# Attention: the products with the greatest score, of four heads in one pass of a step's first set

## The chip, the cores and the metric

The kernel runs on one core of one Trainium2 chip. Its time is device time in microseconds (us), from the start to the end of one execution. The engines of the core work side by side, each through its own list of instructions in order: PE (TensorE, matrix products; its weight loads are shown apart as PEld), DVE (VectorE), ACT (ScalarE), POOL (GpSimd), and SP, which issues most of the DMAs. Matrix products end in PSUM, which has eight banks here of 512 float32 columns by 128 partitions.

## The reference

A small hybrid model, all in float32, for 4 batches of 1024 positions of width 256:

```
x = x + attention(layernorm(x))
x = x + cell(layernorm(x))        # gated recurrence, 64 steps
x = x + deltanet(layernorm(x))
x = x + cell(layernorm(x))

# attention: 16 heads, causal
q_lat = einsum('bqhd,hdl->bhql', q, k_eff)
attn  = softmax(where(causal, einsum('bhql,bkl->bhqk', q_lat, c_kv) / sqrt(hs), -inf))
y     = einsum('bhqk,bkl->bhql', attn, c_kv), then v_eff by heads
```

Only the attention is touched by the change.

## The kernel before, in words

The attention (`attention`, L39 on) fills about the first half of the time, from 19.7 us, when the first scores are multiplied, to about 673 us. What follows it (`feed_and_delta`) is the cell and the deltanet.

The 16 heads of 4 batches are cut into 16 **units** of four heads each (`units`, L66). Each head has 16 numbers to a position; a unit lays its four heads on four row groups of 32 partitions (`rows`, L352). The softmax needs each row's greatest score before the exponentials are taken, so each unit is gone through twice: as `first`, where the scores lie with the queries on the partitions and DVE takes the greatest of each row; and, one unit later, as `second`, where the scores are made again with the keys on the partitions, with the greatest score subtracted by a further product, and ACT takes the exponential out of PSUM into the tile `p`. The loop at L515 runs over i from -1 to 15: unit i+1 is `first` while unit i is `second`. For i from 0 to 14 both are there.

Each round has twelve **steps** (`STEPS`, L52). A step is one block of 128 keys for the one unit, and one block of 128 queries for the other, times n columns: n is 512, 384, 256, 128, then 512 five times, then 384, 256, 128 for the steps 0 to 11. Steps 0 to 3 and 8 to 11 lie on the diagonal. There a product of `identb` and `mb` adds the causal mask for the second unit (L382), and a masked reduction serves the first unit (L407); in steps 4 to 7 the reduction is the plain one at L413.

`quad` (L355) makes a step in two **sets** of four score tiles, one bank each, two of the second unit and two of the first. In this text F0 to F3 are the second unit's tiles of heads 0 to 3 (in the code `False`; "one" is false), whose reader is the exponential on ACT (L403), and T0 to T3 are the first unit's (`True`), whose reader is a reduction on DVE (L407 or L413).

- The first set holds F2, T0, F3, T1; the second F0, T2, F1, T3.
- A set has three **passes** (L384). In the first, each tile gets the product with the high part of the keys (`kh`), in the second that with the low part (`kl`). The four products of a pass lie on four different row groups. In the third pass only the two F tiles get a product, that of `minus` and `gr`, which subtracts the greatest score; in its trace row the products of the second unit are L397 and those of the first unit L388, for all passes.
- Behind the passes stand the four readers (L401 to L415).

Between the two sets of step s stand the products of the exponentials of step s-2 with the values (`values`, L439, matrix products at L447; eight instructions, which use all 128 rows). Behind the second set stand the **woven pieces** (`places`, L525): small parts of other work for PE, each with a tile from the same pool of banks. `greatest` (L423, its product at L427) stands behind steps 0 and 5, `weighed` (L455, four transposes at L461) behind steps 2 and 6. In nine of the rounds pieces of the next batch stand behind steps 1 and 3 to 9: layernorm and `turn` (L232), `latent` (L246), `feature` (L267), `vals` (L256); in some later rounds a few of the next layer's (L232, L343).

All these tiles come from one pool of seven banks (`pss`, L63); the eighth bank holds the values' sum (`pys`). A tile takes a bank that has come free, and the first product into it waits until the reader of the tile that had it is through. The order of the instructions on each engine is the order in which the code stands (`tc.manual_schedule`, L479).

Of the kernel before, what the change touches and what calls it, by code (L numbers as in the profile page):

```python
# [10 lines left out]
F32 = mybir.dt.float32  # L11
BF16 = mybir.dt.bfloat16
F32R = mybir.dt.float32r
AF = mybir.ActivationFunctionType
ALU = mybir.AluOpType
AX = mybir.AxisListType
PSUM = bass.MemoryType.PSUM

P = 128
# [19 lines left out]
def attention(k, w, x):  # L39
# [6 lines left out]
    nc, tc = k.nc, k.tc  # L46
    NT = T // P
    NG = NH // 4
    NU = B * NG
    ROW = HS  # L50

    STEPS = [  # L52
        (3, 0, 512, 0, 0), (2, 0, 384, 0, 1), (1, 0, 256, 0, 2), (0, 0, 128, 0, 3),
        (4, 0, 512, 1, 0), (5, 0, 512, 1, 1), (6, 0, 512, 1, 2), (7, 0, 512, 1, 3),
        (7, 512, 512, 1, 4), (6, 512, 384, 1, 5), (5, 512, 256, 1, 6), (4, 512, 128, 1, 7),
    ]
    with ExitStack() as es:
        wp = es.enter_context(tc.tile_pool(name="a_w", bufs=1))
        big = es.enter_context(tc.tile_pool(name="a_big", bufs=1))
# [2 lines left out]
        pys = es.enter_context(tc.tile_pool(name="a_psy", bufs=1, space=PSUM))  # L62
        pss = es.enter_context(tc.tile_pool(name="a_pss", bufs=7, space=PSUM))  # L63
# [6 lines left out]
        def load(b):  # L70
# [21 lines left out]
        mask = wp.tile([P, 512], F32, name="mask")  # L92
        nc.gpsimd.memset(mask, 0.0)
        nc.gpsimd.affine_select(
            out=mask[:, 384:], in_=mask[:, 384:], compare_op=ALU.is_ge, fill=NEG, base=0,
# [36 lines left out]
        VS = HS + 1  # L132
# [219 lines left out]
        def rows(j):  # L352
            return ds(32 * j, 32)

        def quad(i, s):  # L355


            first = units[i + 1] if i + 1 < NU else None
            second = units[i] if i >= 0 else None
            qt, c0, n, half, kt = STEPS[s]  # L360
            if second is not None:
                p = sm.tile([P, 4, 512], F32, tag="p", name="p", bufs=3)
                second.p[s] = p
                q0 = 512 - n
            if first is not None and s == 0:
                first.m = sm.tile([P, 2, 4, 4], F32, tag="m", name="m")
                first.m0 = sm.tile([P, 4, 4], F32, tag="m0", name="m0")
            kinds = []
            if first is None or second is None:
                kinds.append([(first is not None, j) for j in range(4)])  # L370
            else:
                kinds += [[(False, 2), (True, 0), (False, 3), (True, 1)]]
                kinds += [[(False, 0), (True, 2), (False, 1), (True, 3)]]

            def make(kind):
                tiles = []
                diag = kt >= 4 * half
                for one, j in kind:
                    ps = pss.tile([P, 512], F32, tag="s", name="ps_s1" if one else "ps_s2")
                    tiles.append(ps)  # L380
                    if diag and not one:
                        nc.tensor.matmul(ps[:, 0:P], identb, mb, start=True, stop=True)  # L382
                keys, at = ds(kt * P, P), ds(half * 512 + 512 - n, n)
                for turn_ in range(3):  # L384
                    for (one, j), ps in zip(kind, tiles):
                        r = rows(j)
                        if one and turn_ < 2:
                            nc.tensor.matmul(  # L388
                                ps[:, :n], first.q[r, ds(qt * P, P)], (first.kh, first.kl)[turn_][r, ds(c0, n)],
                                start=turn_ == 0, stop=turn_ == 1,  # L390
                            )
                        elif not one:
                            if turn_ < 2:
                                a, m = (second.kh, second.kl)[turn_][r, keys], second.q[r, at]
                            else:
                                a, m = minus[r, :], second.gr[r, at]
                            nc.tensor.matmul(  # L397
                                ps[:, :n], a, m, start=turn_ == 0 and not diag, stop=turn_ == 2,
                                skip_group_check=diag,
                            )  # L400
                for (one, j), ps in zip(kind, tiles):  # L401
                    if not one:
                        nc.scalar.activation(p[:, j, q0:], ps[:, :n], AF.Exp)  # L403
                        continue
                    if c0 + n == (qt + 1) * P:
                        junk = sm.tile([P, 512], BF16, tag="junk", name="junk")
                        nc.vector.tensor_tensor_reduce(  # L407
                            out=junk[:, :n], in0=ps[:, :n], in1=mask[:, 512 - n :], scale=1.0,
                            scalar=-3e38 if qt < 4 else first.m0[:, j, qt - 4 : qt - 3],
                            op0=ALU.add, op1=ALU.max, accum_out=first.m[:, qt // 4, j, qt % 4 : qt % 4 + 1],  # L410
                        )
                    else:
                        nc.vector.tensor_reduce(  # L413
                            first.m0[:, j, qt - 4 : qt - 3], ps[:, :n], AX.X, ALU.max
                        )  # L415

            make(kinds[0])
            yield
            for kind in kinds[1:]:
                make(kind)  # L420
            yield

        def greatest(i, half):  # L423
# [14 lines left out]

        def values(i, s):  # L439
            u = units[i]  # L440
            _, _, n, half, kt = STEPS[s]
            q0 = 512 - n
            last = kt == 4 * half + 3
            if kt == 0:
                u.y = pys.tile([P, 512], F32, tag="y", name="ps_y")
            for j in range(4):
                nc.tensor.matmul(  # L447
                    u.y[ds(32 * j, 32), q0:], vb[u.b % 2][:, kt, ds((4 * u.g + j) * VS, 32)], u.p[s][:, j, q0:],
                    start=kt == 0, stop=last,
                )  # L450
            if last:
                u.ys = sm.tile([P, 512], F32, tag="ys", name="ys")
                nc.scalar.copy(u.ys, u.y)  # L453
# [24 lines left out]
        LAG = 2  # L478
        with tc.manual_schedule():  # L479
# [35 lines left out]
            for i in range(-1, NU):  # L515

                if i >= 0 and i % NG == 0 and i // NG + 1 < B:
                    rest += of_batch(i // NG + 1)
                if i > NG and i % NG == 1:

                    late += normed(i // NG - 1, True)
                if i == NG + 1:
                    late.append(k.scale_ffn)
                    late += [lambda g=g: first_cells(g) for g in "fic"]
                places = [[] for _ in range(12)]  # L525
                if i < 0:
                    places[0] += rest[:2]
                    places[1] += rest[2:4]
                    for a, f in enumerate(rest[4:]):
                        places[3 + a * 9 // len(rest[4:])].append(f)  # L530
                    rest = []
                else:
                    for work, left in ((rest, NG - 1 - i % NG), (late, NG - i % NG)):
                        share = -(-len(work) // left) if left > 0 else len(work)
                        for a, f in enumerate(work[:share]):
                            places[LONG[a * len(LONG) // share]].append(f)
                        del work[:share]
                if i + 1 < NU:
                    places[5].append(lambda i=i: greatest(i + 1, 0))
                if 0 <= i < NU - 2:  # L540

                    for j in range(4):
                        places[2 + j].append(lambda i=i, j=j: heads(i + 2, j))
                if i >= 0:
                    units[i].p = {}
                    places[0].insert(0, lambda i=i: greatest(i, 1))
                    places[6].insert(0, lambda i=i: weighed(i, 0))
                if i >= 1:
                    places[2].insert(0, lambda i=i: weighed(i - 1, 1))
                for s in range(12):  # L550
                    run = quad(i, s)
                    next(run)
                    at = i * 12 + s - LAG
                    if at >= 0:
                        values(*divmod(at, 12))
                    next(run)
                    for f in places[s]:
                        f()
                if i == 1:
                    k.load_ffn()  # L560
                if i == NG + 2:
                    load(B - 1)
            for at in range(NU * 12 - LAG, NU * 12):
                values(*divmod(at, 12))
            weighed(NU - 1, 1)


# [1034 lines left out]
```

## Time and profile before

| | |
|---|---|
| median of 3 runs | 1350.02 us (1347.22 to 1359.29) |
| the profiled execution | 1350.2 us |
| its span, first to last instruction | 1348.4 us |
| TensorE clock granted in it | 0.985 of full speed on average, 1.00 from 110 to 600 us |
| busy in the span: PE, DVE, ACT, POOL | 1276.7, 851.0, 708.4, 422.3 us |
| busy between 300 and 400 us, in the attention: PE, DVE, ACT, POOL | 98.91, 75.66, 63.57, 20.94 us |
| DMA, share of 16 engines between 300 and 400 us | 0.31 |

Busy PE is not PE at its peak: products on different row groups run side by side, and the time of one, with its way through the array, counts as busy. So in the attention a PE that is 99% busy still contains waits, and they show as idle time ahead of its weight loads. The profile's page gives the busy times, forty slices of the span, the chain of work that ended last and the groups of instructions by line; the timeline gives the start of each instruction.

### The profile page before, as it was taken

To read this page: it belongs to the slowest core of one execution; us is meant where nothing else is said; L and a number is where in the kernel's file an instruction comes from. 1 tells how busy PE (TensorE), PEld (TensorE's weight loads), DVE (VectorE), ACT (ScalarE), POOL (GpSimd) and SP (SyncE) were. 2 spreads that over 40 slices of the span, in tenths; PEclk is the share of its full clock that TensorE was granted. 3 is DMA by queue.
4 is the path that set the end of the run, shared out by engine and by line. 5 is a ranking of instruction groups with operands and counts; after the bars stand their busy time and mean duration, and the time that the engine had idled before them with its cause. 6 is when DMAs were issued, how large, how long until landed. Compare 5 with 4: busy or idle time off the path is not lost. (4 is left out here: it accounts for less than half of the span.)

```text
span 1348.4 us, 36845 instructions
## 1 busy us (share of the span) xinstructions
PE 1276.7 (95%) x14596; PEld 773.9 (57%) x14596; DVE 851.0 (63%) x2440; ACT 708.4 (53%) x1754; POOL 422.3 (31%) x681
## 2 busy tenths in 40 slices
PE   7899999999999999999899989989888999999997
PEld 3444454444554444444444766756555677777886
DVE  6776778777787777788122345467978867434333
ACT  3266666566666666666732366445565543334332
POOL 1040002323032020022000136445888844535220
PEclk9799999999999999999999999989999999999999
DMA  3723712334221233220030123313555432333210
GB/s 111 187 50 81 198 50 61 60 88 144 66 54 50 97 92 66 66 50 4 25 97 6 47 63 90 102 40 110 139 145 137 132 99 71 106 90 100 63 63 32
DMA packets 118652, 112.25 MB, mean 83 GB/s; under 512 B 46672, under 2 KB 103504, under 8 KB 118480
## 3 DMA queue, kind: packets, MB, share of 16 engines
q1 hardware_dynamic: 95200, 100.39, 27.7%
q10 hardware_dynamic: 23280, 9.51, 2.7%
q8 instruction: 115, 1.88, 0.6%
q14 instruction: 57, 0.47, 0.1%
HBM read 65.22 MB, written 44.63 MB: 81 GB/s over the span
## 5 line engine op out<-in xcount | busy, mean ns | idle before, releaser
L403 ACT ACTIVATE p<-ps_s 128x512 f32<-128x512 f32 (+3 forms) x768 | 334.4, 491 | 209.6 <-PE ps_s L397 208.3
L388 PE MATMUL ps_s<-kh,q 32*128 32x512 f32 (+3 forms) x768 | 220.9, 438 | 10.0 <-DMA q<-qall 4.7
L413 DVE TENSOR_REDUCE m<-ps_s 128x1 f32<-128x512 f32 x256 | 163.8, 682 | 26.3 <-PE ps_s L388 26.1
L397 PE MATMUL ps_s<-q,kh 32*128 32x512 f32 (+3 forms) x768 | 176.9, 438 | 0.0
L388 PE MATMUL ps_s<-kl,q 32*128 32x512 f32 (+3 forms) x768 | 169.7, 358 | 0.0
L447 PE MATMUL ps_y<-p,vb 128*32 128x512 f32 (+3 forms) x1536 | 164.1, 500 | 1.4 <-ACT ys L453 1.4
L407 DVE CUSTOM_DVE_ANT_0 junk<-ps_s,mask,m 128x512 bf16<-128x512 f32 (+3 forms) x256 | 129.2, 547 | 48.7 <-PE ps_s L388 36.4
L407 DVE CUSTOM_DVE_ANT_0 junk<-ps_s,mask 128x512 bf16<-128x512 f32 (+3 forms) x256 | 114.6, 486 | 45.4 <-PE ps_s L388 39.1
L397 PE MATMUL ps_s<-q,kl 32*128 32x512 f32 (+3 forms) x768 | 143.0, 370 | 0.0
L397 PE MATMUL ps_s<-gr,minus 32*128 32x512 f32 (+3 forms) x768 | 132.2, 343 | 0.0
L388 PEld LDWEIGHTS ps_s<-kh,q 32*128 32x128 f32 x768 | 100.1, 182 | 43.3 <-DVE m L413 14.3
L397 PEld LDWEIGHTS ps_s<-q,kh 32*128 32x128 f32 x768 | 76.9, 182 | 83.0 <-ACT p L403 20.7
L471 POOL TENSOR_TENSOR xa<-xa,yt 128x256 f32<-128x256 f32 x32 | 23.4, 732 | 277.9 <-DVE yt L467 266.4
L382 PEld LDWEIGHTS <-identb 128*128 128x128 bf16 x512 | 34.6, 98 | 104.0 <-issue 98.7
L388 PEld LDWEIGHTS ps_s<-kl,q 32*128 32x128 f32 x768 | 87.9, 185 | 0.0
L194 POOL TENSOR_SCALAR rs<-mv 128x2 f32<-128x2 f32 x24 | 5.5, 228 | 256.6 <-DVE mv L193 256.6
L1079 DVE SCALAR_TENSOR_TENSOR gate<-gate 128x256 f32<-128x256 f32 (+1 forms) x56 | 29.3, 523 | 77.1 <-ACT gate L1058 77.1
L397 PEld LDWEIGHTS ps_s<-gr,minus 32*128 32x128 f32 x768 | 73.4, 185 | 3.2
L382 PE MATMUL ps_s<-mb,identb 128*128 128x128 bf16 x512 | 72.1, 224 | 0.8 <-ACT vb L257 0.3
L397 PEld LDWEIGHTS ps_s<-q,kl 32*128 32x128 f32 x768 | 71.5, 184 | 0.0
L1039 PE MATMUL ps_gate<-xnT,ffn_wi 128*128 128x256 f32 (+1 forms) x224 | 67.1, 423 | 3.5 <-DVE hh L1152 3.3
L1039 PE MATMUL ps_gate<-xnT,ffn_wf 128*128 128x256 f32 (+1 forms) x224 | 66.9, 422 | 1.3 <-DVE yt L467 1.0
(228 smaller groups left out, 2607.1 us busy)
## 6 DMA issues: line engine op xcount, KB each, us to landing
x<-x SPq DMA_DIRECT2D x30, 512.0 KB
kh<-kall SPq DMA_DIRECT2D x120, 64.0 KB
kl<-kall SPq DMA_DIRECT2D x120, 64.0 KB
q<-qall SPq DMA_DIRECT2D x120, 64.0 KB
kall<-hl SPq DMA_DIRECT2D x14, 512.0 KB
qall<-hl SPq DMA_DIRECT2D x12, 512.0 KB
kept<-gs ACTq DMA_DIRECT2D x32, 192.0 KB
gl<-kept SPq DMA_DIRECT2D x32, 192.0 KB
```

Source lines behind the costliest of these rows:

```text
L194: nc.gpsimd.tensor_scalar(rs, mv[:, :, 1], EPS, None, ALU.add)
L382: nc.tensor.matmul(ps[:, 0:P], identb, mb, start=True, stop=True)
L388: nc.tensor.matmul(ps[:, :n], first.q[r, ds(qt * P, P)], (first.kh, first.kl)[turn_][r, ds(c0, n)], start=turn_ == 0, stop=turn_ == 1,)
L397: nc.tensor.matmul(ps[:, :n], a, m, start=turn_ == 0 and not diag, stop=turn_ == 2, skip_group_check=diag,)
L403: nc.scalar.activation(p[:, j, q0:], ps[:, :n], AF.Exp)
L407: nc.vector.tensor_tensor_reduce(out=junk[:, :n], in0=ps[:, :n], in1=mask[:, 512 - n :], scale=1.0, scalar=-3e38 if qt < 4 else first.m0[: ...
L413: nc.vector.tensor_reduce(first.m0[:, j, qt - 4 : qt - 3], ps[:, :n], AX.X, ALU.max)
L447: nc.tensor.matmul(u.y[ds(32 * j, 32), q0:], vb[u.b % 2][:, kt, ds((4 * u.g + j) * VS, 32)], u.p[s][:, j, q0:], start=kt == 0, stop=last,)
L471: nc.gpsimd.tensor_tensor(xs, xs, yt.rearrange("p n j d -> p n (j d)"), ALU.add)
L1039: nc.tensor.matmul(ps, f["w" + "fic"[j]][:, kc, ds(m * P, P)], k.xnT[:, kc, t, ds(at, width)], start=kc == 0, stop=t == 0 and kc == KC - 1,)
L1079: nc.vector.scalar_tensor_tensor(acts[1], acts[1], 1.0, acts[2], ALU.add, ALU.mult)
```

## The change

In rounds where both units are there, the third pass of the first set now holds the products with `gr` of all four heads: F2 and F3, whose other two products have just been made, and F0 and F1, whose tiles are opened for it. F0 and F1 then stay open over the values' products. In the second set they get their mask and their products with `kh` and `kl`, which add to what is there, and the set ends behind two passes. The number of products is the same. The first set opens six tiles, the second T2 and T3. The readers keep their order: F2, T0, F3, T1 behind the first set and F0, T2, F1, T3 behind the second. Rounds with one unit alone keep their three (or two) passes.

On diagonal steps the tiles of F2 and F3 are now asked for ahead of T0 and T1, since both masks stand ahead of the first pass.

The rest of the diff changes the form and not the work: a step is a list of pieces, with one piece in each list; `p` is filled from column 0 and not from column 512-n, and `values` reads it there.

```diff
-    STEPS = [
-        (3, 0, 512, 0, 0), (2, 0, 384, 0, 1), (1, 0, 256, 0, 2), (0, 0, 128, 0, 3),
...
+        [(3, 0, 512, 0, 0)], [(2, 0, 384, 0, 1)], [(1, 0, 256, 0, 2)], [(0, 0, 128, 0, 3)],
...
-            kinds = []
-            if first is None or second is None:
-                kinds.append([(first is not None, j) for j in range(4)])
-            else:
-                kinds += [[(False, 2), (True, 0), (False, 3), (True, 1)]]
-                kinds += [[(False, 0), (True, 2), (False, 1), (True, 3)]]
...
-            make(kinds[0])
-            yield
-            for kind in kinds[1:]:
-                make(kind)
+            open_ = {}
+
+            def bank(one, j):
+                if (one, j) not in open_:
+                    open_[one, j] = pss.tile([P, 512], F32, tag="s", name="ps_s1" if one else "ps_s2")
+                return open_[one, j]
+
+            def masks(js):
+                if diag:
+                    for j in js:
+                        ps = bank(False, j)
+                        for x, (at, _, _, _, _, _) in enumerate(pieces):
                             nc.tensor.matmul(
+                                ps[:, ds(at, P)], identb, mb, start=x == 0 and (False, j) not in begun, stop=True,
+                                skip_group_check=True,
                             )
...
+            def product(one, j, turn_, last):
+                ps, r = bank(one, j), rows(j)
+                for x, (at, qt, c0, n, half, kt) in enumerate(pieces):
+                    if one:
+                        a, m = first.q[r, ds(qt * P, P)], (first.kh, first.kl)[turn_][r, ds(c0, n)]
+                    else:
+                        cols = ds(half * 512 + 512 - n, n)
+                        if turn_ < 2:
+                            a, m = (second.kh, second.kl)[turn_][r, ds(kt * P, P)], second.q[r, cols]
+                        else:
+                            a, m = minus[r, :], second.gr[r, cols]
+                    nc.tensor.matmul(
+                        ps[:, ds(at, n)], a, m, start=x == 0 and (one, j) not in begun, stop=last,
+                        skip_group_check=True,
+                    )
+                begun.add((one, j))
...
+            else:
+                masks((2, 3))
+                for turn_ in range(2):
+                    for one, j in ((False, 2), (True, 0), (False, 3), (True, 1)):
+                        product(one, j, turn_, one and turn_ == 1)
+                for j in (2, 3):
+                    product(False, j, 2, True)
+                for j in (0, 1):
+                    product(False, j, 2, False)
+                for one, j in ((False, 2), (True, 0), (False, 3), (True, 1)):
+                    finish(one, j)
+                yield
+                masks((0, 1))
+                for turn_ in range(2):
+                    for one, j in ((False, 0), (True, 2), (False, 1), (True, 3)):
+                        product(one, j, turn_, turn_ == 1)
+                for one, j in ((False, 0), (True, 2), (False, 1), (True, 3)):
+                    finish(one, j)
             yield
...
-                    u.y[ds(32 * j, 32), q0:], vb[u.b % 2][:, kt, ds((4 * u.g + j) * VS, 32)], u.p[s][:, j, q0:],
+                        u.y[ds(32 * j, 32), q0:], vb[u.b % 2][:, kt, ds((4 * u.g + j) * VS, 32)],
+                        u.p[s][:, j, ds(at, n)], start=kt == 0, stop=last,
```

## The prediction

> **What bounds the kernel.** I read the page's busy times first, then the forty slices, then the waits of the score products, then the timeline of one step. The page and its slices:
>
> ```profile
> PE 1276.7 (95%) x14596; PEld 773.9 (57%) x14596; DVE 851.0 (63%) x2440; ACT 708.4 (53%) x1754; POOL 422.3 (31%) x681
> ...
> PE   7899999999999999999899989989888999999997
> ...
> DVE  6776778777787777788122345467978867434333
> ACT  3266666566666666666732366445565543334332
> ```
>
> The first 20 slices are the attention: PE full, DVE at 7, ACT at 6. That looks as if a pass taken from PE were a pass saved. But a product's way through the array counts as busy, so waits hide in it. The waits of the second unit's products (source view of L397):
>
> ```profile
> L397 PE MATMUL ps_s<-gr,minus x768: 267/382/624, 56.2 to 669.7; 32*128 32x512 f32 x96, 32*128 32x384 f32 x32, 32*128 32x256 f32 x32, 32*128 32x128 f32 x32
> ...
> its engine sat idle before it (us, times) until:
>   ACT p L403: 20.7, 29
>   DVE m L413: 16.7, 36
> ```
>
> PE's weight loads wait for the readers of older tiles, and the source view of L388 adds 16.3 us for L413 and 12.5 us for L407: 66 us in 150 waits. PE is bounded by its passes and by banks coming free, in turns. The timeline of round 12, from the second set of step 7 to the values' products of step 8, shows how:
>
> ```profile
> 560.63 0.49 PE L397 MATMUL ps_s<-q,kh 32*128 32x512 f32 x1
> ...
> 560.97 0.39 PE L397 MATMUL ps_s<-q,kl 32*128 32x512 f32 x1
> ...
> 561.20 0.40 PE L397 MATMUL ps_s<-gr,minus 32*128 32x512 f32 x2
> 561.40 1.29 DVE L413 TENSOR_REDUCE m<-ps_s 128x1 f32<-128x512 f32 x2 [0.23 <-PE ps_s L388]
> 561.53 0.29 PE L382 MATMUL ps_s<-mb,identb 128*128 128x128 bf16 x2
> 561.62 1.09 ACT L403 ACTIVATE p<-ps_s 128x512 f32<-128x512 f32 x2 [0.77 <-PE ps_s L397]
> ...
> 562.14 0.49 PE L388 MATMUL ps_s<-kh,q 32*128 32x512 f32 x1
> ...
> 562.48 0.40 PE L397 MATMUL ps_s<-gr,minus 32*128 32x512 f32 x2
> ```
>
> I count from 560.63. The passes start at 0, 0.34 and 0.57, the next product on all rows at 0.90: a third pass is worth 0.23. The reductions start at 0.77; one takes 0.68, the two 1.29, so T2 is read at 1.45, T3 at 2.06. The exponentials start at 0.99 (one 0.60, both 1.09): F0 is read at 1.59, F1 at 2.08. The next first set starts at 1.11 with three tiles, and its fourth, T1, only at 1.51, 0.06 after T2's reduction. From there it is 0.34 to the last pass and 0.33 to the values' products: 2.18. So of seven banks the second set holds four, three are free, and the fourth tile waits for the first that is read. Where one tile is woven in between, the third waits for T2 and the fourth for F0 (behind step 5, 555.57, F0's end 555.51). Banks come free as T2, F0, T3, F1.
>
> **The change, part by part.** *Removed:* the second set's third pass, 0.23 at 512 columns and, by the same spacing in round 12, 0.18 at 384, 0.11 at 256, 0.12 at 128. A round has six, two, two and two of these: 2.2 us, 33 us over the 15 rounds with both units. Rounds with one unit stay.
>
> *Costed at nothing:* the first set's third pass with four products instead of two. It hides in the row groups, as the second pass does, whose four products start within 0.01 and last 0.39 each. If they ran one pair after the other, the 33 us were gone. The masks keep form and number (0.22), `p` its widths, and SP's and POOL's queues are passed by nothing. The set already read `gr` for F2 and F3, so no DMA is needed earlier. T3 of the second set still takes the bank of T0's reduction, as it does now.
>
> *Added:* the first set wants six banks, with four held by the set before. So F0 waits for the second reader, F1 for the third (for the fourth, where a tile is woven in between). Behind that wait stand, in PE's order, the values' products and the whole second set. Which reader is third no row shows: after the change T2 and F0 end their products together. If exponentials, the shorter, are released in turn with reductions, the order is F0, T2, F1, T3 and F1 is third; if the present order stays, T3 is. I take F1, and keep T3 for the range.
>
> The same boundary after: exponentials start at 0.76, F0 is read at 1.36, F1 at 1.85, T2 and T3 as before. T1 starts at 1.42, its last pass at 1.76. F1's product loads at 1.85 + 0.06, streams 0.10 later (0.34 less 0.23 or so between passes is the load) and is followed after 0.32: values at 2.33 instead of 2.18, **0.15 later**. The pass is saved and a longer wait stands in its place. The same working at each boundary of a round, from the timeline of rounds 0 to 14:
>
> - No tile between, wide enough to wait (30 times: behind steps 1, 4, 7, 8, 9 in rounds without woven batch work): +0.12 to +0.15, in sum **+4.2**.
> - Behind step 0, `greatest` between (15): T3 is fourth, read at 2.07; 384 columns follow in 0.37, so 2.50 against 2.245: **+3.8**.
> - Behind steps 10, 11, 2, 3 (about 53; small n): +0.05, -0.09, -0.11, -0.02: **-2.5**.
> - One short tile between (`weighed` alone, or a turn; 10 that count): T3 at 2.06 + 0.48 = 2.54 against 2.40, up to +0.24 at 384: **+1.6**. Turns behind steps 4 and 8 of rounds 0, 4 and 8 wait for their own input: 0.
> - One long tile between (L246 1.85, L267 0.96, L256 0.97; about 34): all banks are read by then, the pass is saved, -0.12 to -0.24: **-6.3**.
> - Two or more tiles between (some 20: behind steps 5 and 6, and scattered): the sixth bank is the woven tile's own. `weighed`'s is read only when L467 ends, 2.75 in, so values at 3.23, where 2.81 (round 11), 3.08 (rounds 0, 4, 8) or 3.24 stand now; a `feature` tile's when L275 ends, about 3.1 to 3.8 in. From 0 to +0.6: **+4.6**.
>
> Sum: **+5.4 us** on the profiled execution's 1350.2 (span 1348.4 and 1.8 around it; the median of the runs is 1350.02): 1355.6.
>
> One page of the Trainium skill speaks against the change: TensorEngine Tiling (Array Packing), PSUM Bottleneck, says that packing speeds up TensorE but not the emptying of PSUM, which may then become the bottleneck. The row above it is T1's wait of 0.40 for a reduction. By that rule alone the saved pass would be worth nothing at every boundary and the time stay at 1350; the rows say more (a gain behind long tiles, a loss elsewhere).
>
> **The rivals.** *The banks come in time.* If F0's and F1's banks cost no wait, T1's remains: 1.42 + 0.67 = 2.09, 0.09 less than now, at the 30 plain boundaries (-2.7), -0.1 behind steps 0 and 10 (-3), -2.9 at the other small ones, -1.5 behind short tiles, -6.3 behind long ones, -0.24 at 16 with several (-3.8): -20, **1330**. For it: 66 us of waits are not the whole attention, and DVE is at 75.66 of 100 us between 300 and 400. Against it: F1's exponential, at 1.85, is 0.09 behind the start of the pass that needs its bank, even if all else is early. The limit is 33 us, 1317.
>
> *T3 is third (slower).* One mechanism: the order in which banks come free stays T2, F0, T3, F1, so F1's product waits for the second reduction. At 45 boundaries without a tile between (the 30 and those behind step 10) that ends 0.2 to 0.3 later than F1's exponential (2.06 against 1.85 at 512, 1.81 against 1.53 at 384, 1.43 against 1.20 at 256): 45 x 0.26 = 12 us more, **1367**. It decides as soon as the second reduction is the third reader. For it: this order stands in the trace. Against it: it stands there because the T tiles are ready a pass before the F tiles, and that lead is what the change takes away.
>
> *It doesn't do what it says:* the four third products run in pairs. Then the saving is none and the waits stay, about +30, 1380. Four products side by side in the second pass speak against it.
>
> **How the numbers follow.** Mine 0.62, banks in time 0.13, T3 third 0.22, pairs 0.03. Mine alone reaches from 1346 to 1364, since the boundaries with several tiles are read from single rounds (half or double 4.6) and the load of 0.10 may be hidden (45 x 0.10). Two in ten are left out between 1338 and 1370, the first cut into the early-banks case, the second past T3's. One per cent is 13.5 us, about what a measurement of this kernel can tell from no change. Faster than 1336.5 is the early-banks case, a little less than all: 0.12. Slower than 1363.5 is T3 third, pairs and the end of mine, less the part of T3's that falls short: 0.24. The rest, 0.64.
>
> **What would show it.** Second sets at 512 columns 0.67 long instead of 0.90; exponentials there 0.2 earlier; idle time ahead of the weight loads of the `gr` products with ACT's p as releaser (with DVE's m, if T3 is third); values' products 2.3 after the second set's start where nothing is between (2.1: banks in time; 2.55: T3); rounds 1, 2, 5, 6, 9 and 10 shorter by about 0.5 to 1 us or unchanged, rounds 3 and 12 longer by 0.9. I am wrong if the wait moves to T1, if a woven tile's reader is later than I read, or if DVE, with less idle time, falls behind in steps 4 to 7.

## The result, and the profile after

The changed kernel takes **1357.03 us** (median of 20 runs, 1354.24 to 1361.59); the kernel before took 1349.12 in 20 runs beside them (1344.09 to 1359.29). The ratio is 1.0046, with a 95% interval of 1.0025 to 1.0067: slower by less than one per cent, 7.9 us in the medians and some 6 by this ratio. The prediction's sum was 1355.6. The profiled execution after took 1358.04 us, its span 1356.2; before, 1350.2 and 1348.4.

The page after, its busy times and two of the slice rows (PE and DVE; a digit is the busy share of one fortieth of the span in tenths):

```profile
PE 1281.8 (95%) x14596; PEld 778.4 (57%) x14596; DVE 846.4 (62%) x2440; ACT 709.9 (52%) x1754; POOL 423.1 (31%) x681
...
PE   7899999999999999999999989989888999999997
...
DVE  5776777777776777777322345377887867534333
```

PE runs the same 14596 products and is busy 5 us longer: waiting products count as busy, so this page alone tells nothing of a saved pass. DVE is busy no longer than before (846.4 against 851.0 us, the same 2440 instructions) and has not become the bound. Between 300 and 400 us, at a granted clock of 1.00 in both, DVE is busy 72.05 us instead of 75.66 and ACT 60.25 instead of 63.57.

The waits of the score products (source view of L410, which records the products of both units; releaser, us in all, times):

```profile
its engine sat idle before it (us, times) until:
  issue: 46.8, 93
  ACT p L419: 35.6, 98
  DVE m L430: 11.5, 28
  DVE m L424: 7.4, 17
```

Before, ACT's exponentials released 22 us of such waits and DVE's reductions 46; now it is 36 and 19. The releaser has moved from DVE to ACT: the exponentials have become the first and the third reader of the second set. The shift is larger than these sums say. Thirty of the waits in each kernel, 25 us together, stand right behind the values' products and last 0.84 each; before, the view puts 12.6 us of them to ACT and 8.4 to DVE, and after, all of them to "issue" (where the engine waited for nothing that the profile shows).

The boundary that the prediction shows, round 12 from the second set of step 7 to the values' products of step 8, in the timeline after (start, duration, engine, line, operation; in brackets the idle time ahead and what ended it):

```profile
569.70 0.49 PE L410 MATMUL ps_s<-q,kh 32*128 32x512 f32 x1
...
570.38 0.28 PE L391 MATMUL ps_s<-mb,identb 128*128 128x128 bf16 x2
570.47 1.09 ACT L419 ACTIVATE p<-ps_s 128x512 f32<-128x512 f32 x2 [0.83 <-PE ps_s L410]
570.50 1.29 DVE L430 TENSOR_REDUCE m<-ps_s 128x1 f32<-128x512 f32 x2 [0.39 <-PE ps_s L410]
...
571.12 0.18 PEld L410 LDWEIGHTS ps_s<-kh,q 32*128 32x128 f32 x1 [0.34 <-ACT p L419]
...
571.46 0.65 PE L410 MATMUL ps_s<-gr,minus 32*128 32x512 f32 x4
571.61 0.18 PEld L410 LDWEIGHTS ps_s<-gr,minus 32*128 32x128 f32 x1 [0.18 <-ACT p L419]
...
572.03 0.64 PE L488 MATMUL ps_y<-p,vb 128*32 128x512 f32 x4
```

The prediction's rows of the same boundary before, from 560.63, end with this one:

```profile
562.81 0.16 PEld L447 LDWEIGHTS ps_y<-p,vb 128*32 128x32 f32 x8 [0.37 <-issue]
```

From 569.70: the mask of the next first set comes at 0.68 where it came at 0.90, so the pass is saved. The exponentials start at 0.77; F0 is read at 1.36, and T1's weights load 0.06 later, at 1.42, released by ACT's `p`. F1 is read at 1.86 and the last third product's weights load at 1.91, again released by `p`. The values' products come at 2.33 instead of 2.18.

**Where the time lies.** I compared each stretch from one step's values' products to the next step's, rounds 0 to 14, in the two profiled executions. They add up to about +10 us: from the first values' products to those of round 15, 578.0 us before and 587.9 after. The span grew by less, 7.8, for reasons outside the change: the first values' products already come 1.9 us later, in a prologue of the same work at a lower clock (0.92 between 14 and 58 us, against 0.96 between 14 and 56 before), while behind the attention two stretches of the same work run 1.8 and 2.8 us shorter (685.7 to 766.5 us at a granted clock of 1.00, before 673.8 to 756.4 at 0.98; and 864.0 to 924.8 at 0.97, before 853.9 to 917.5 at 0.92).

The sum of these stretches, against the kernel before, is called "boundaries" below. The profiled executions of e1, e3 and e4 each have one short stretch of the attention at half the clock (granted 0.51 from 508.9 to 512.3 us in e1, 0.50 from 602.6 to 609.4 in e3 and from 596.7 to 600.1 in e4), behind steps 5 and 6 of round 11 or 13. There these kernels are 1.3 to 2.6 us longer than before, and the slower clock, not the edit, is the main part of it. So these four stretches (behind steps 5 and 6 of both rounds) are left out of the sum in every kernel; the change has +9.8 by this count.

| Boundary, by what is woven in between | predicted, us | measured, us |
|---|---|---|
| nothing, wide (30) | +4.2 | +3.65 |
| behind step 0, `greatest` (15; 14 compared) | +3.8 | +4.0 |
| behind steps 10, 11, 2, 3 | -2.5 | +2.5 |
| one short tile | +1.6 | +2.7 |
| one long tile (34) | -6.3 | -5.3 |
| two or more tiles, and `greatest` behind step 5 | +4.6 | +2.7 |
| sum | +5.4 | +10.2 |

The table counts from each second set's start, all stretches included. What it has over the 9.9 lies in round 0, where the clock was halved until 69.9 us before and until 71.1 after.

### The profile page after: what moved, and what is told of

Same layout as the page of the kernel before. It is cut to its first block, busy times and chain, and to the rows that moved or that the text cites. A ratio compares the mean times of both kernels' runs of the same rounds, so it can differ in the third digit from the quotient of the medians.

```text
span 1356.2 us, 36841 instructions
## 1 busy us (share of the span) xinstructions
PE 1281.8 (95%) x14596; PEld 778.4 (57%) x14596; DVE 846.4 (62%) x2440; ACT 709.9 (52%) x1754; POOL 423.1 (31%) x681
## 5 line engine op out<-in xcount | busy, mean ns | idle before, releaser
L410 PE MATMUL ps_s<-kh,q 32*128 32x512 f32 (+3 forms) x768 | 214.6, 440 | 9.3 <-DMA q<-qall 3.3
L410 PE MATMUL ps_s<-q,kh 32*128 32x512 f32 (+3 forms) x768 | 178.4, 438 | 2.2 <-ACT p L419 2.2
L410 PE MATMUL ps_s<-kl,q 32*128 32x512 f32 (+3 forms) x768 | 164.1, 359 | 0.0
L410 PE MATMUL ps_s<-q,kl 32*128 32x512 f32 (+3 forms) x768 | 143.4, 366 | 0.0
L410 PEld LDWEIGHTS ps_s<-q,kh 32*128 32x128 f32 x768 | 77.2, 183 | 85.7 <-issue 41.8
L410 PEld LDWEIGHTS ps_s<-kh,q 32*128 32x128 f32 x768 | 96.1, 183 | 40.3 <-ACT p L419 16.9
L410 PE MATMUL ps_s<-gr,minus 32*128 32x512 f32 (+3 forms) x768 | 104.8, 362 | 1.3 <-DVE hl L286 1.1
L410 PEld LDWEIGHTS ps_s<-kl,q 32*128 32x128 f32 x768 | 85.9, 187 | 0.0
L410 PEld LDWEIGHTS ps_s<-gr,minus 32*128 32x128 f32 x768 | 69.5, 185 | 14.5 <-DVE hl L286 2.3
L410 PEld LDWEIGHTS ps_s<-q,kl 32*128 32x128 f32 x768 | 72.2, 185 | 0.0
L1080 PE MATMUL ps_gate<-xnT,ffn_wc 128*128 128x256 f32 (+1 forms) x224 | 66.2, 418 | 1.1 <-ACT gate L1099 0.6
```

The lines of the kernel that those rows point to most:

```text
L410: nc.tensor.matmul(ps[:, ds(at, n)], a, m, start=x == 0 and (one, j) not in begun, stop=last, skip_group_check=True,)
L1080: nc.tensor.matmul(ps, f["w" + "fic"[j]][:, kc, ds(m * P, P)], k.xnT[:, kc, t, ds(at, width)], start=kc == 0, stop=t == 0 and kc == KC - 1,)
```

## The experiments

The third line of the table is the miss. Behind step 3 the values' products come 0.19 later than before, and behind step 11 0.07 later, where the prediction had a little sooner: yet banks come early there, since the tiles read last are small. In the rows of step 3 something else is late (first the end of this boundary before, whose second set starts at 549.01, then the timeline after, from the second set's start at 557.58):

```profile
550.18 0.40 PE L397 MATMUL ps_s<-gr,minus 32*128 32x512 f32 x2
550.51 0.16 PEld L447 LDWEIGHTS ps_y<-p,vb 128*32 128x32 f32 x8 [0.36 <-issue]
```

```profile
558.49 0.41 PEld L410 LDWEIGHTS ps_s<-gr,minus 32*128 32x128 f32 x4
...
558.72 0.39 PE L410 MATMUL ps_s<-kl,q 32*128 32x512 f32 x1
558.73 0.62 PE L410 MATMUL ps_s<-gr,minus 32*128 32x512 f32 x4
...
559.27 0.64 PE L488 MATMUL ps_y<-p,vb 128*32 128x256 f32 x8
```

Four third products take 0.62 together, 0.22 more than the 0.40 of products that run side by side. No bank wait is recorded in front of the last of them, and all four readers of the second set are through by 1.01. T1 starts late for its bank, so its second product (`kl,q`) starts at 1.14, together with the third pass. It lies on row group 1 (the 32 partitions of head 1). F1's third product lies on the same row group and starts 0.22 behind it. So there are two theories of the lost time: **banks** (F0's and F1's third products wait for two more readers) and **row group** (F1's product queues behind the late T1's second product, whatever the banks). At 512 columns they price the same boundary alike, 2.33 and 1.42 + 0.34 + 0.23 + 0.32 = 2.31.

**e1: the third products of F0 and F1 left out.** The first set opens four banks as before the change, the second has two passes; with the greatest score not subtracted, the exponential's scale is 0.

```
-   for j in (0, 1):
-       product(False, j, 2, False)
-   nc.scalar.activation(p[...], ps[...], AF.Exp)
+   nc.scalar.activation(p[...], ps[...], AF.Exp, scale=0.0)
```

> Leaves out the third product of F0 and F1 altogether (so their scores lack the greatest score, and the exponential is taken of zero times the score): the second set has two passes and the first set wants four banks, as before the change. Both theories expect the same, the size of the saved pass where no bank is added: T1 starts at 1.42 behind the second set's start (F0 read at 1.36) and the values' products follow 0.67 later, at 2.09, behind step 7 of round 12 (before 2.18, after the change 2.33); 0.24 less behind long woven pieces. Time about 1330, 1.4% below the kernel before.

Measured: 1332.61 us, ratio 0.9899 (0.9874 to 0.9923) against 1346.76 before on the same chip; boundaries -17.0 us. The timeline of the same boundary:

```profile
549.80 0.50 PE L410 MATMUL ps_s<-q,kh 32*128 32x512 f32 x1
...
551.21 0.18 PEld L410 LDWEIGHTS ps_s<-kh,q 32*128 32x128 f32 x1 [0.20 <-ACT p L419]
...
551.55 0.40 PE L410 MATMUL ps_s<-gr,minus 32*128 32x512 f32 x2
551.88 0.64 PE L486 MATMUL ps_y<-p,vb 128*32 128x512 f32 x4
```

T1 starts at 1.41 as after the change, the two third products end the set, and the values' products come at 2.08. So a pass saved without any price is worth 14 us here (17 at the boundaries), and not the 33 us of passes removed: behind step 7 the values' products come 0.10 sooner and not 0.23, since T1 still waits for F0's bank. And what the change lost against this, 26.8 us at the boundaries, is the price of where the two products went.

**e2: as e1, and in their place T0's and T1's second product once more, in their own banks.** The third pass again has four products, one of them on T1's row group, but no bank is wanted that T0 and T1 don't already have.

```
-   for j in (0, 1):
-       product(False, j, 2, False)
+   for j in (0, 1):
+       product(True, j, 1, True)
```

> As e1, but the first set's third pass has four products again: beside F2's and F3's, T0 and T1 get their low product a second time, into their own banks (so the first unit's scores are wrong by that). The row groups carry what they carry after the change, the banks are four as before it. Theory of banks (the last product waits for F1's bank): values' products at 2.09 as in e1, about 1330. Theory of the row group (T1 starts late for its own bank, and the third product on T1's row group queues behind T1's second): three passes behind T1, 1.42 + 0.34 + 0.23 + 0.32 = 2.31 behind step 7 of round 12, 1.69 behind step 3, about 1343.

Measured: 1336.89 us, ratio 0.9925 (0.9899 to 0.9951); boundaries -7.9 us. The same boundary:

```profile
552.22 0.49 PE L410 MATMUL ps_s<-q,kh 32*128 32x512 f32 x1
...
553.63 0.18 PEld L410 LDWEIGHTS ps_s<-kh,q 32*128 32x128 f32 x1 [0.34 <-ACT p L419]
...
553.97 0.39 PE L410 MATMUL ps_s<-kl,q 32*128 32x512 f32 x1
...
554.21 0.39 PE L410 MATMUL ps_s<-kl,q 32*128 32x512 f32 x1
...
554.52 0.64 PE L488 MATMUL ps_y<-p,vb 128*32 128x512 f32 x4
```

T1's repeated product starts at 554.21, 0.24 behind its second one, with no bank to wait for, and the values' products come at 2.30, not at 2.08. The row group alone makes a fourth pass of it. Behind step 3 it gives 1.69, exactly what the change gives. But at 384 and 256 columns it doesn't reach the change's times (behind steps 9 and 10 of round 12, 1.74 and 1.45 against 1.89 and 1.50), and its whole time stays below the change's, by 16 us as the two ratios have it and 17.7 at the boundaries. So the row group is real, and not the main part.

**e3: the banks opened early, the pass not saved.** F0 and F1 are opened in the first set by 32 columns of their third product; the other columns stay in a third pass of the second set, as before the change.

```
+   for j in (0, 1):
+       product(False, j, 2, False, hi=32)      # first set, third pass
...
+   for j in (0, 1):
+       product(False, j, 2, True, lo=32)       # second set, third pass
```

> The other part alone: F0 and F1 are opened in the first set, as after the change, but with 32 columns of their third product only; the other columns follow in a third pass of the second set, as before the change. Nothing is left out. No pass is saved, six banks are wanted. Theory of banks: F1 is read at 2.08 as before the change, so the small product starts at 2.14 and the values' products at about 2.36 behind step 7 of round 12 (before 2.18); about 1364. Theory of the row group: the small product costs about 0.03 behind T1's second, 2.2; 1350 to 1353.

Measured: 1367.26 us, ratio 1.0152 (1.0123 to 1.0181); boundaries +15.1 us. The same boundary, which starts at 572.12:

```profile
573.63 0.18 PEld L411 LDWEIGHTS ps_s<-kh,q 32*128 32x128 f32 x1 [0.22 <-DVE m L432]
...
574.23 0.18 PEld L411 LDWEIGHTS ps_s<-gr,minus 32*128 32x128 f32 x1 [0.29 <-DVE m L432]
574.43 0.16 PEld L492 LDWEIGHTS ps_y<-p,vb 128*32 128x32 f32 x8
```

With the third pass back in the second set the reductions lead again. T1 waits for T2's reduction, as before the change, and F1's product waits for T3's, which ends at 574.17: this is the order T2, F0, T3, F1 of the second rival. Only 32 columns have to follow there, so the values' products come at 2.31, 0.13 later than before; behind steps 8 and 9 they come 0.33 and 0.31 later. Behind steps 3 and 11 nothing is lost (1.51 and 1.60 against 1.50 and 1.60): so short a product doesn't hold up its row group. So two banks wanted earlier, with two short products more in a step and no pass saved, cost 20.5 us in the medians and 15.1 at the boundaries.

**e4: the change, with T1's second product left out.** T1 has one pass, so nothing of it stands before F1's product on row group 1; the banks are wanted as in the change.

```
-       product(one, j, turn_, one and turn_ == 1)
+       if turn_ == 0 or (one, j) != (True, 1):
+           product(one, j, turn_, one and (turn_ == 1 or j == 1))
```

> The kernel after, with T1's second product left out (the first unit's scores of head 1 lack the low part of the keys), so that row group 1 has two products behind T1's start, not three. Banks stay as after the change. Theory of banks: behind step 7 of round 12 the values' products stay at 2.33, and fall only where T1 is last (behind steps 3 and 11, from 1.69 to about 1.48): 1352. Theory of the row group: 1.42 + 0.34 + 0.32 = 2.09 behind step 7; about 1343.

Measured: 1354.04 us, ratio 1.0052 (1.0034 to 1.0070); boundaries +5.1 us. First the boundary behind step 7, from 565.77, then the one behind step 3, from 553.89:

```profile
567.52 0.65 PE L410 MATMUL ps_s<-gr,minus 32*128 32x512 f32 x4
567.67 0.18 PEld L410 LDWEIGHTS ps_s<-gr,minus 32*128 32x128 f32 x1 [0.18 <-ACT p L419]
...
568.11 0.64 PE L489 MATMUL ps_y<-p,vb 128*32 128x512 f32 x4
```

```profile
555.03 0.40 PE L410 MATMUL ps_s<-gr,minus 32*128 32x512 f32 x4
...
555.36 0.64 PE L489 MATMUL ps_y<-p,vb 128*32 128x256 f32 x8
```

Behind step 7 nothing changes: the last of the four still loads at 1.90, when F1's exponential is through, they still take 0.65, and the values' products come at 2.33 (2.34 by the rounded rows). Behind step 3 the four now take 0.40 together, and the values' products come at 1.47 instead of 1.69; behind step 11 at 1.49 instead of 1.68. There the prediction had 1.48 and 1.51.

The four kernels form a square. Boundaries against the kernel before, in us, and round 12's values' products, counted from the second set's start:

| | before | neither (e1) | row group (e2) | banks (e4) | both (the change) |
|---|---|---|---|---|---|
| sum | 0 | -17.0 | -7.9 | +5.1 | +9.8 |
| behind step 7 (512 columns) | 2.18 | 2.08 | 2.30 | 2.33 | 2.33 |
| behind step 0 (`greatest`, 384) | 2.25 | 2.14 | 2.27 | 2.53 | 2.53 |
| behind step 9 (384, then 256) | 1.78 | 1.63 | 1.74 | 1.89 | 1.89 |
| behind step 11 | 1.60 | 1.48 | 1.69 | 1.49 | 1.68 |
| behind step 3 | 1.50 | 1.47 | 1.69 | 1.47 | 1.69 |

Each of these five boundaries takes the later of the two, within 0.02. In the sums, banks alone cost 22.1 us over e1; the row group adds 4.7 to that, and it would cost 9.1 without them.

**e5: the new order only where a long piece is woven in.** In steps 2 to 5 and 7 to 10 of rounds 1, 2, 5, 6, 9 and 10, with a few exceptions and two steps of round 7; elsewhere the order of before. This leaves nothing out.

```
+               if early:
                    for j in (0, 1):
                        product(False, j, 2, False)
...
-                        product(one, j, turn_, turn_ == 1)
+                        product(one, j, turn_, turn_ == 1 and (one or early))
+                if not early:
+                    for j in (0, 1):
+                        product(False, j, 2, True)
```

> Chooses by step: F0's and F1's third products stand in the first set only where the first set follows a woven piece that is long enough for the banks to be read (rounds 1, 2, 5, 6, 9 and 10, steps 2 to 5 and 7 to 10, without two boundaries with two tiles; round 7, steps 5 and 9), or follows weighed at step 3; in all other steps the order is that of the kernel before. Nothing is left out. If the saved pass is paid back by the wait for banks and by the row group behind T1, and only where nothing long stands between, this keeps the gains (about 34 boundaries, 0.12 to 0.24 each, and the pass that step 5 saves) and none of the losses: 7 to 8 us below the kernel before, ratio 0.994 to 0.995, and below the kernel after by twice that. If the loss comes from something else in the new order, it stays near the kernel before.

Measured: 1347.73 us in 12 runs against 1347.57 in 17, ratio 0.9994 (0.9971 to 1.0018): no difference that can be measured, and less than I expected. In its profile the rounds in the old order agree with before to 0.02 at round 12's steps, and the boundaries sum to -4.6 us, some -3.5 of them at the long pieces; 4.6 us would be a ratio of 0.9966, just outside the interval. The expectation was too high because the saved pass is not a gain in every one of these sets: in step 5 T3's bank waits for T0's reduction, so T3 starts 0.25 late and the set is no shorter, and behind `weighed` or two tiles some lost 0.05 to 0.32. The clock hides a part of the gain, as far as the runs tell: the granted clock was below 0.985 in 7 of these 12 runs and in 3 of the 17 before, and the others average 1344.6 and 1347.2 us. That would be a gain of 2 to 3 us at the same clock; whether the new order itself draws the clock down is not shown. By the medians, no version that does the whole work beats the kernel before by a measurable amount.

## Why the prediction was right or wrong, point by point

- **The saved pass and the four products in one pass: right.** Second sets at 512 columns are 0.67 to 0.68 long ahead of the mask. Where the banks are free (e4, step 3), the four take 0.40, as one does; "they run in pairs" falls.
- **The choice of F1 as third: right.** T1 loads at 1.42 and the last third product's weights at 1.91, both released by ACT's `p`, as reckoned. "T3 is third" falls; in e3, where the F tiles again have a pass more than the T tiles, it does happen, so the reason against it (the T tiles lose their lead) was the right one.
- **No tile between, wide: right, and only nearly for the reason given.** 2.33 as forecast; e4 shows that the banks alone hold it there. e2 shows that without them it would be 2.30.
- **Behind steps 10, 11, 2 and 3: wrong, and the largest error.** The step that failed is the path of T1, "1.42 + 0.67": its last pass at T1 + 0.34 and the values' products 0.33 behind it. With F1's third product on T1's row group it is T1 + 0.34 + 0.23 + 0.32 = T1 + 0.89. Steps 3 and 11 measured +0.19 and +0.07 a boundary instead of -0.02 and -0.09 (+1.7 and +1.0 us); step 10 +0.035 (+0.5, forecast +0.05); behind step 2 the gain was real but smaller (-0.76 over 14). Together 5 us of the sum.
- **"The banks come in time", 1330: not as priced.** The same 0.67 stands in it. With the row group, e2 gives 1337; only e1, which doesn't make the products at all, gets below that.
- **One short tile: mis-sized.** `weighed` behind step 6 and the turns behind step 9 came as worked out (up to +0.24). The turns behind step 8 of rounds 0, 4 and 8 were put at 0 because they wait for their own input; they lost 0.33 each, 1.0 us in all. T3 is read at 2.40 there, and F1's product, which wants its bank, leaves the values' products at 2.92 instead of 2.58.
- **One long tile: right in sign, -5.3 against -6.3.**
- **Two or more tiles: a range with the right ends, its value too high.** In three boundaries behind step 5 (rounds 2, 6, 10) the fourth product waits for the feature tile's last reader, as foreseen, at +0.5 to +0.9. The timeline of round 2, from 162.18:

```profile
165.39 0.40 PE L410 MATMUL ps_s<-gr,minus 32*128 32x512 f32 x3
...
166.19 0.18 PEld L410 LDWEIGHTS ps_s<-gr,minus 32*128 32x128 f32 x1 [0.83 <-DVE hl L286]
...
166.61 0.16 PEld L488 LDWEIGHTS ps_y<-p,vb 128*32 128x32 f32 x8 [0.24 <-issue]
```

  Three products side by side, the fourth 0.80 later, and the values' products behind it. But behind step 6 of rounds 0, 4 and 8 the values' products came 0.22 sooner, where 0.15 later (3.23 against 3.08) was worked out: the last third product there loads long before `weighed`'s reader ends, so the bank it got was not the woven tile's.
- **The sum.** +5.4 forecast, +10.2 at the boundaries of the profiled executions, +7.9 in the medians. That the forecast of 1355.6 lies 1.4 us from the median is luck in part: the row group is missing from it, and the terms for long tiles and for several tiles err in both directions. By rounds it was less good: rounds 3 and 12 grew by 1.3 us and not 0.9, and rounds 2 and 10, forecast to be shorter or unchanged, grew by 0.4 and 0.3. In the six pairs the boundaries of one execution and the medians differ by about 2 to 5 us. The clock is a likely part of it: the runs of e1, e3, e4 and e5 had a median granted clock of 0.983 to 0.985, those before beside them 0.987, and these are the four whose medians lie above their boundaries (0.003 of 1348 us is 4 us, an estimate; no run holds the clock fixed). For e2 and the change the rest of 2 us has the other sign and stays open. DVE did not fall behind in steps 4 to 7, as feared: between 300 and 400 us it was busy less than before.
- **The packing rule.** The Trainium skill, TensorEngine Tiling (Array Packing), PSUM Bottleneck, was weighed as "the saved pass is worth nothing, 1350". The rule is borne out as to where the limit lies, since e3's wanted banks cost 15.1 us at the boundaries with no pass saved. It gives no size, and the change is worse than nothing saved.

## What to carry to other kernels

A product that opens an accumulator earlier also claims a bank earlier, and all that is queued behind it waits for one reader more: list the banks in the order in which their readers end before moving it. Then list the row groups in issue order, since a tile that starts late for its bank holds up the next product on its row group by a whole pass, even where that product's own bank has long been free. Where a woven piece outlasts the readers, the saved pass is a gain; where none is woven in, the readers take it back.

## What I had not expected of the hardware

Products on different row groups that start together take 0.40 us together at 512 columns, but one product on an occupied row group adds 0.22 to 0.24 (0.62 against 0.40 behind step 3, 554.21 against 553.97 in e2), and it holds up the next product on all rows by as much. The Trainium skill, TensorE: Matmul & The Clock Gate, The mechanism, says that products start and end strictly in order, and the starts in these rows agree (the ends are modelled). It also says that weights are loaded beside products in flight only where the row group differs. The trace shows otherwise. Behind step 3 the last of the four `gr` loads, F1's, starts at 558.72 (558.49 + 0.41 - 0.18), where T1's product on the same row group starts too, and F1's own product follows at 558.95 (558.73 + 0.62 - 0.40). Behind step 7 F1's weights load at 571.61, 0.15 after T1's product has started there. By these starts the load lies beside the product, and behind step 3 the wait is for the row group itself. The same section's earlier sentence, that a load can also run ahead into a background weight buffer, fits these rows.

The granted clock differed between single executions by 0.02 to 0.05 in stretches that the change doesn't touch, worth 1.8 and 2.8 us there, beside 7.9 us for the whole effect. In the attention it shows as short stretches at half the clock, 3.4 us long in e1 and e4 and 6.8 in e3. Stretches bounded by the same products told the two apart.
